# State sums by accumulating DMAs, a third of the C products off VectorE, and a new order of pieces in a tuned scan-and-attention kernel

## The chip, the cores and the metric

The kernel runs on one core of a Trainium2 chip. The metric is the device time of one execution in microseconds (us). A kernel's time is the median of its runs, with the lowest and highest beside it. Engines are named as in the profile: PE is TensorE, PEld its weight loads, DVE is VectorE, ACT is ScalarE, POOL is GpSimd, and SP is SyncE, which here only issues transfers.

## The reference, cut to what matters

The input is 4 images of 4096 positions with 96 channels. One block follows another:

```python
# layer 0: a selective scan with 16 states per channel
x = x + conv(GroupNorm(x))
#   xf = LayerNorm(...) * gamma + beta
#   value, gate, delta, A, B, C = split(xf @ W_in + b_in)   # A, B, C: 96 x 16 columns each
#   h = d * A * h + d * B * u          (d = delta, u = value, along the 4096 positions)
#   y = sigmoid(gate) * sum over 16 states (C * h);   y @ W_out + b_out
# layer 1: linear attention and a feed-forward net, rounded to 8 and 16 bit floats
t = t + attention(LayerNorm(t));  t = t + ffn(LayerNorm(t))
```

The kernel cuts an image into 8 chunks of 512 positions, and a chunk into 12 tiles of 128 (channel, state) pairs: 4 sets of states by 3 groups of 32 channels. One tile is one step, so there are 32 chunks and 384 steps.

## The kernel before

Each step has a fixed core, and the other work ("pieces") is dealt out to the 12 positions of a chunk.

```python
# one step s (cut): A, B, C projections on PE; B's copy on ACT and product on POOL;
# A's product, the scan and C's product on DVE
tiles[s + 1].a_proj();  tiles[s].c_proj();  last.keep()
tiles[s + 1].b_mul()                       # POOL
last = tiles[s];  last.scan()              # DVE
tiles[s + 1].a_mul()                       # DVE
last.c_mul()                               # DVE
call(s)                                    # the pieces dealt to this step
tiles[s + 2].b_proj();  tiles[s + 2].b_copy()
...
# state_sum (cut): 4 sets x 3 groups x 2 passes of a matmul with a folding matrix, one set every 3 steps
# LayerNorm (cut): a product of 128 x 4 elements on DVE, both inputs in SBUF
nc.vector.scalar_tensor_tensor(nmr, self.mv[:, :, 0], -1.0, self.r, ALU.mult, ALU.mult)
...
# front (cut): x is split into a high part xs and a rest lo; lo reads PSUM and one SBUF input
nc.scalar.activation(v["xs"][0:C, :], v["ps"], AF.Copy, scale=gam)
nc.vector.scalar_tensor_tensor(lo, v["ps"], gam, v["xs"][0:C, :].bitcast(F32), ALU.mult, ALU.subtract)
...
# tail (cut): the transposed chunk, 97 rows of 512, stays in SBUF until attention a whole image later
xat[b, i] = big.tile([CA, J, P], F32, tag="xat", name=f"xat_{nm}", bufs=NCH + 2)
nc.scalar.copy(xat[b, i], v["ps"])
```

An image's x is loaded once and kept, also for the GroupNorm of the image that comes next.

Of the kernel before, what the change touches and what calls it, by code (L numbers as in the profile page):

```python
# [38 lines left out]
GN0, GN_EVERY = 22, 6  # L39
FFN0 = 15  # L40
XBUFS = 2 * NCH + 5
# [4 lines left out]
def conv_attn_hybrid_kernel(  # L46
# [27 lines left out]
    psum = ctx.enter_context(tc.tile_pool(name="psum", bufs=1, space=PSUM))  # L74

    BANKS = {"A": 2, "B": 1, "C": 1, "Y": 1, "M": 2, "G": 1}

    def bank(tag, shape, name):
        return psum.tile(shape, F32, tag=tag, name=name, bufs=BANKS[tag])

# [8 lines left out]
    xt = {}  # L89

    def load_x(b, i):
        t = big.tile([P, J, C], F32, tag="x", name=f"x_{b}_{i}", bufs=XBUFS)
        nc.sync.dma_start(t, x_v[b, i])
        xt[b, i] = t
# [3 lines left out]


# [4 lines left out]
    raw0 = big.tile([C, A0], F32, tag="x", name="raw0", bufs=XBUFS)  # L104
    nc.scalar.dma_start(raw0, w_in[:, 0:A0])
    raws, brows = {}, {}
    for k, c0 in enumerate((B0, A0, C0)):
        for cg in range(NCG):
            t = big.tile([C, 32 * S], F32, tag="xat", name=f"raw{k}{cg}", bufs=NCH + 2)
            n0 = c0 + cg * 32 * S  # L110
            nc.scalar.dma_start(t, w_in[:, n0 : n0 + 32 * S])
            raws[k, cg] = t
        brows[k] = work.tile([NCG, 32 * S], F32, tag="ch", name=f"brow{k}", bufs=6)
        nc.scalar.dma_start(
            brows[k], b_in[c0 : c0 + C * S].rearrange("(g n) -> g n", g=NCG)
        )
    b_dug = const.tile([C, 3], F32, name="b_dug")
    for k in range(3):
        nc.scalar.dma_start(b_dug[:, k : k + 1], b_in[k * C : (k + 1) * C].unsqueeze(1))

# [24 lines left out]






    def split_high(dst, src):

        nc.scalar.copy(dst[0:C, 0], src)

    def split_low(dst, src, engine):
        engine.tensor_tensor(dst[0:C, 1], src, dst[0:C, 0].bitcast(F32), ALU.subtract)

    def split_copies(dst):
        v = dst.bitcast(F32)
        nc.sync.dma_start(v[C:P, 0], v[64:C, 0])  # L160
        nc.sync.dma_start(v[C:P, 1], v[64:C, 1])
        nc.sync.dma_start(v[0:64, 2], v[0:64, 0])
        nc.sync.dma_start(v[64:P, 2], v[0:64, 1])

    def split_rows(xs, xl, lo):

        nc.sync.dma_start(xl[0:64, :].bitcast(F32), lo[0:64, :].bitcast(F32))
        nc.sync.dma_start(xl[64:P, :].bitcast(F32), lo[0:64, :].bitcast(F32))
        nc.sync.dma_start(xs[C:P, :].bitcast(F32), lo[64:C, :].bitcast(F32))

    def project(ps, wt, split):

        xs, xl = split
        for n, mv in enumerate((xs, xs, xl)):
            nc.tensor.matmul(ps, lhsT=wt[:, n], rhs=mv, start=(n == 0), stop=(n == 2))  # L175


    bets = const.tile([P, 2], F32R, name="bets")
    betl = const.tile([P, 2], F32R, name="betl")
    betlo = const.tile([C, 2], F32R, name="betlo")  # L180
    nc.scalar.copy(bets[0:C, :], bet.to_broadcast([C, 2]))
    nc.gpsimd.tensor_tensor(
        betlo, bet.to_broadcast([C, 2]), bets[0:C, :].bitcast(F32), ALU.subtract
    )
    split_rows(bets, betl, betlo)

    w_dug = const.tile([P, 3, 3 * C], F32R, name="w_dug")
    split_high(w_dug, raw0)
    split_low(w_dug, raw0, nc.gpsimd)
    split_copies(w_dug)  # L190
    w_bac = [const.tile([P, 3, NCG, NSH * P], F32R, name=f"w_{k}") for k in range(3)]
    b_bac = const.tile([P, 3, NCG, NSH], F32, name="b_bac")

    def cols(k, cg):

        return (
            w_bac[k][:, :, cg].rearrange("k n (s c) -> k n s c", s=S),
            raws[k, cg].rearrange("k (c s) -> k s c", s=S),
        )

    def high(k):
        for cg in range(NCG):
            split_high(*cols(k, cg))

    def low(k, engine):
        for cg in range(NCG):
            split_low(*cols(k, cg), engine)
        split_copies(w_bac[k].rearrange("k n g c -> k n (g c)"))

    def bias_dug():  # L210
        ps = bank("Y", [C, 3, 2], "dug_ps")
        for k in range(3):
            project(ps[:, k], w_dug[:, :, k * C : (k + 1) * C], (bets, betl))
        nc.vector.tensor_tensor(b_dug, b_dug, ps[:, :, 0], ALU.add)


    betd = []
    for nm, t in (("s", bets), ("l", betl)):
        m = const.tile([P, NCG, 4], F32R, name=f"betd_{nm}")
        nc.gpsimd.memset(m.bitcast(F32), 0.0)  # L220
        for cg in range(NCG):
            nc.gpsimd.tensor_copy(m[:, cg, cg : cg + 1], t[:, 0:1].bitcast(F32))
        betd.append(m)

    def bias(k):
        ps = bank("Y", [4, NSH * P], f"bias_ps{k}")
        for cg in range(NCG):
            for n, t in enumerate((betd[0], betd[0], betd[1])):
                nc.tensor.matmul(
                    ps, lhsT=t[:, cg, :], rhs=w_bac[k][:, n, cg],  # L230
                    start=(cg == 0 and n == 0), stop=(cg == NCG - 1 and n == 2),
                )
        row = work.tile([NCG, NSH * P], F32, tag="ch", name=f"bias{k}", bufs=6)
        nc.vector.tensor_tensor(
            row.rearrange("g (s c) -> g s c", s=S),
            ps[0:NCG].rearrange("g (s c) -> g s c", s=S),
            brows[k].rearrange("g (c s) -> g s c", s=S), ALU.add,
        )
        t_ps = bank("C", [P, NSH, NCG], f"biast_ps{k}")
        for sh in range(NSH):  # L240
            nc.tensor.transpose(
                t_ps[:, sh, :], row[:, sh * P : (sh + 1) * P], ident[:NCG, :NCG]
            )
        nc.vector.tensor_copy(b_bac[:, k], t_ps.rearrange("p h g -> p g h"))


    w_o = const.tile([CA, C], F32, name="w_o")
    nc.scalar.dma_start(w_o[0:C, :], w_out)
    nc.scalar.dma_start(w_o[C:CA, :], b_out.unsqueeze(0))
    w_qkv = const.tile([CA, 3 * C], F32, name="w_qkv")  # L250
    nc.scalar.dma_start(w_qkv[0:C, :], wqkv)
    nc.scalar.dma_start(w_qkv[C:CA, :], bqkv.unsqueeze(0))
    w_ff = const.tile([C, C], F32, name="w_ff")
    nc.scalar.dma_start(w_ff, wff)

    w_qt = const.tile([CA, CA], F32, name="w_qt")
    kvff = const.tile([CA, C], F32, name="kvff")
    nc.scalar.dma_start(kvff[C:CA, :], bff.unsqueeze(0))
    w1_q = const.tile([C, HID], F8, name="w1_q")
    w2_q = const.tile([P, NK, C], F8, name="w2_q")  # L260
    b1_q = const.tile([P, NK], F32, name="b1_q")
    b2_q = const.tile([P, C], F32, name="b2_q")
    w1_sb = big.tile([P, NK, C], F32, tag="x", name="w1_sb", bufs=XBUFS)
    nc.scalar.dma_start(w1_sb, w1.rearrange("(m p) k -> p m k", p=P))
    w2_sb = big.tile([C, HID], F32, tag="x", name="w2_sb", bufs=XBUFS)
    nc.scalar.dma_start(w2_sb, w2)
    b1_sb = big.tile([NK, P], F32, tag="x", name="b1_sb", bufs=XBUFS)
    nc.scalar.dma_start(b1_sb, b1.rearrange("(m p) -> m p", p=P))
    b2_sb = big.tile([P, C], F32, tag="x", name="b2_sb", bufs=XBUFS)
    nc.scalar.dma_start(b2_sb, b2.partition_broadcast(P))  # L270

    def weights_attention():
        nc.gpsimd.memset(w_qt[C:CA, :], 0.0)
        nc.gpsimd.memset(w_qt[C:CA, C:CA], 1.0)
        ps = bank("Y", [C, CA], "wq_ps")
        nc.tensor.transpose(ps, w_qkv[:, 0:C], ident[:CA, :CA])
        nc.vector.tensor_copy(w_qt[0:C, :], ps)

    def weights_ffn1():
        ps = bank("Y", [C, HID], "w1_ps")  # L280
        for m in range(NK):
            nc.tensor.transpose(ps[:, m * P : (m + 1) * P], w1_sb[:, m, :], ident)
        nc.vector.tensor_copy(w1_q, ps, saturate=False)

    def weights_ffn2():
        ps = bank("Y", [P, NK, C], "w2_ps")
        for m in range(NK):
            nc.tensor.transpose(ps[:, m, :], w2_sb[:, m * P : (m + 1) * P], ident[:C, :C])
        nc.vector.tensor_copy(w2_q, ps, saturate=False)

    def weights_bias():
        ps = bank("Y", [P, NK], "b1_ps")
        nc.tensor.transpose(ps, b1_sb, ident[:NK, :NK])
        b1_8 = small.tile([P, NK], F8, tag="b1_8", name="b1_8", bufs=1)
# [10 lines left out]
    for r in range(2):  # L305
        t = const.tile([P, J, CA], F32, tag=f"xa{r}", name=f"xa{r}")
        nc.gpsimd.memset(t[:, :, C:CA], 1.0)
        xa_t.append(t)


    fold = const.tile([P, 32], F32, name="fold")

    hmask = []

# [611 lines left out]
```

## Time and profile before

| | before |
|---|---|
| median of 3 runs | 1439.53 us (1438.23 to 1440.04) |
| span of the profiled run, granted TensorE clock | 1435.1 us, 0.951 |
| first scan starts | 71.1 us |
| last scan starts, time from there to the end | 1347.5 us, 88 us |
| transfers that PE waits for inside the loop | none |

A group line reads: line, engine, operation, output<-inputs, shapes, count, then busy us in all and mean ns of one, then the idle time of the engine just before these instructions and who ended it. The prediction below shows the main groups. Two groups of DVE instructions that it doesn't show matter later:

```profile
L521 DVE SCALAR_TENSOR_TENSOR lo<-xnt_ps,gam,xs 96x512 fp32r<-96x512 f32 x32 | 23.6, 738 | 1.6 <-ACT xs L516 1.6
L350 DVE SCALAR_TENSOR_TENSOR nmr_c<-mv_c,rstd_c 128x4 f32<-128x4 f32 x32 | 5.4, 169 | 1.0 <-POOL rstd_c L328 1.0
```

The first takes 738 ns for 512 columns and has one of its two large inputs in PSUM (xnt_ps). The second takes 169 ns for 4 columns, with both inputs in SBUF.

### The profile page before, as it was taken

To read this page: it belongs to the slowest core of one execution; us is meant where nothing else is said; L and a number is where in the kernel's file an instruction comes from. 1 tells how busy PE (TensorE), PEld (TensorE's weight loads), DVE (VectorE), ACT (ScalarE), POOL (GpSimd) and SP (SyncE) were. 2 spreads that over 40 slices of the span, in tenths; PEclk is the share of its full clock that TensorE was granted. 3 is DMA by queue.
4 is the path that set the end of the run, shared out by engine and by line. 5 is a ranking of instruction groups with operands and counts; after the bars stand their busy time and mean duration, and the time that the engine had idled before them with its cause. 6 is when DMAs were issued, how large, how long until landed. Compare 5 with 4: busy or idle time off the path is not lost. (4 is left out here: it accounts for less than half of the span.)

```text
span 1435.1 us, 20740 instructions
## 1 busy us (share of the span) xinstructions
PE 1300.3 (91%) x6396; PEld 891.0 (62%) x6396; DVE 1212.5 (84%) x2309; ACT 723.1 (50%) x1658; POOL 747.2 (52%) x743
## 2 busy tenths in 40 slices
PE   2699988899999899899999998989999999999885
PEld 2356665666666666666666666666666666666562
DVE  2398988899998898899998888889999999999742
ACT  3234343433336555555555455665554555655555
POOL 3254544455554555555555555555556566545424
PEclk6699999999999999999999999999999999999955
DMA  6422222222222222222222122222222222222001
GB/s 156 107 61 56 49 55 61 48 54 54 54 59 51 69 51 56 57 47 60 60 50 70 45 62 57 58 52 58 59 49 49 51 60 59 50 49 51 12 6 44
DMA packets 81357, 80.98 MB, mean 56 GB/s; under 512 B 49617, under 2 KB 50101, under 8 KB 81246
## 3 DMA queue, kind: packets, MB, share of 16 engines
q1 hardware_dynamic: 78544, 77.22, 22.6%
q10 hardware_dynamic: 2702, 2.43, 0.7%
q8 instruction: 51, 0.84, 0.3%
q14 instruction: 60, 0.49, 0.1%
HBM read 8.72 MB, written 6.29 MB: 10 GB/s over the span
## 5 line engine op out<-in xcount | busy, mean ns | idle before, releaser
L598 POOL TENSOR_TENSOR bu<-bu,du 128x512 f32<-128x512 f32 x384 | 493.9, 1286 | 575.2 <-ACT bu L595 351.2
L614 DVE TENSOR_TENSOR_SCAN h<-Aps,state,bu 128x512 f32<-128x512 f32 x336 | 428.1, 1274 | 46.6 <-POOL bu L598 45.4
L595 ACT ACTIVATE bu<-Bps,b_bac 128x512 f32<-128x512 f32 x384 | 261.8, 682 | 398.2 <-PE Bps L175 386.2
L607 DVE SCALAR_TENSOR_TENSOR Aps<-Aps,b_bac,d 128x512 f32<-128x512 f32 x384 | 284.3, 740 | 64.5 <-PE Aps L175 63.8
L175 PE MATMUL Bps<-xs,w 128*128 128x512 f32 x768 | 271.0, 434 | 52.7 <-ACT gx_ps L412 37.6
L632 DVE SCALAR_TENSOR_TENSOR ch<-Cps,b_bac,h 128x512 f32<-128x512 f32 x384 | 285.5, 744 | 1.5 <-PE Cps L175 1.3
L175 PE MATMUL Cps<-xs,w 128*128 128x512 f32 x768 | 245.0, 401 | 3.0 <-DVE ch L632 2.9
L175 PE MATMUL Aps<-xs,w 128*128 128x512 f32 x768 | 241.7, 396 | 2.4 <-DVE h L614 2.1
L175 PEld LDWEIGHTS Bps<-xs,w 128*128 128x128 f32 x768 | 127.4, 191 | 102.1 <-ACT gx_ps L412 44.8
L175 PEld LDWEIGHTS Cps<-xs,w 128*128 128x128 f32 x768 | 142.1, 190 | 46.4 <-DVE ch L632 17.9
L175 PEld LDWEIGHTS Aps<-xs,w 128*128 128x128 f32 x768 | 145.4, 190 | 38.0 <-DVE h L614 4.1
L175 PE MATMUL Bps<-xl,w 128*128 128x512 f32 x384 | 152.6, 397 | 0.0
L175 PE MATMUL Aps<-xl,w 128*128 128x512 f32 x384 | 151.9, 395 | 0.0
L175 PE MATMUL Cps<-xl,w 128*128 128x512 f32 x384 | 151.6, 395 | 0.0
L645 PE MATMUL y_ps<-ch,fold 128*32 128x512 f32 x768 | 136.5, 605 | 0.0
L354 ACT ACTIVATE xa<-x,nmr_a,rstd_a 128x96 f32<-128x96 f32 x128 | 49.4, 457 | 105.0 <-DVE nmr_a L350 105.0
L354 ACT ACTIVATE z<-z,nmr_c,rstd_c 128x96 f32<-128x96 f32 x128 | 49.4, 457 | 78.1 <-DVE nmr_c L350 78.1
L175 PEld LDWEIGHTS Aps<-xl,w 128*128 128x128 f32 x384 | 72.8, 190 | 16.9
L175 PEld LDWEIGHTS Bps<-xl,w 128*128 128x128 f32 x384 | 72.6, 189 | 16.9
L175 PEld LDWEIGHTS Cps<-xl,w 128*128 128x128 f32 x384 | 72.8, 189 | 16.5
L787 ACT ACTIVATE hq<-hr 128x512 fp8e5<-128x512 f16 x96 | 60.6, 631 | 17.9 <-PE y_ps L793 8.2
L614 DVE TENSOR_TENSOR_SCAN h<-Aps,bu 128x512 f32<-128x512 f32 x48 | 58.1, 1211 | 11.0 <-POOL bu L598 10.9
(163 smaller groups left out, 1594.3 us busy)
## 6 DMA issues: line engine op xcount, KB each, us to landing
d<-d SPq DMA_DIRECT2D x384, 64.0 KB, 2.0
du<-du SPq DMA_DIRECT2D x384, 64.0 KB, 2.0
xl<-lo SPq DMA_DIRECT2D x64, 128.0 KB, 2.3
x<-in_x_dram SPq DMA_DIRECT2D x32, 192.0 KB, 2.8
out_dram<-o SPq DMA_DIRECT2D x32, 192.0 KB, 2.2
w<-w SPq DMA_DIRECT2D x6, 384.0 KB
xs<-lo SPq DMA_DIRECT2D x32, 64.0 KB, 2.0
raw<-in_L_conv_W_in_dram ACTq DMA_DIRECT2D x9, 192.0 KB, 4.5
```

The source lines that it names most:

```text
L175: nc.tensor.matmul(ps, lhsT=wt[:, n], rhs=mv, start=(n == 0), stop=(n == 2))
L354: nc.scalar.activation(dst[:, j, 0:C], src[:, j, :], AF.Identity, bias=nmr[:, j : j + 1], scale=self.r[:, j : j + 1],)
L595: nc.scalar.activation(self.bu, self.b_ps, AF.Identity, bias=self.bias(0))
L598: nc.gpsimd.tensor_tensor(self.bu, self.bu, rep["du4", self.b, self.i, self.cg], ALU.mult)
L607: nc.vector.scalar_tensor_tensor(self.a_ps, self.a_ps, self.bias(1), rep["d4", self.b, self.i, self.cg], ALU.add, ALU.mult,)
L614: nc.vector.tensor_tensor_scan(self.h, self.a_ps, self.bu, 0.0 if self.i == 0 else state[self.sh, self.cg], ALU.mult, ALU.add,)
L632: nc.vector.scalar_tensor_tensor(self.ch, self.c_ps, self.bias(2), self.h, ALU.add, ALU.mult)
L645: nc.tensor.matmul(y_ps[g][cg * 32 : (cg + 1) * 32, :], lhsT=fold, rhs=tiles.pop(g * NT + NCG * sh + cg).ch, start=(sh == 0), stop=(sh == ...
L787: nc.scalar.activation(v["hq"][:, m, :], v["hr", m], AF.Copy, saturate=False)
```

## The change

The intent is to take work off the two engines that are nearly full. State sets are added by DMA instead of by PE, four of twelve C products move from DVE to ACT and POOL, and the pieces are dealt anew. To make room in SBUF for the larger C tiles, two things that had stayed in SBUF now travel: x is loaded twice (once for GroupNorm as `gx`, once for the rest), and the transposed chunk `xat` is written to memory and read back. The diff, cut to its core:

```diff
+ON_POOL = (1, 3, 6, 10)
-XBUFS = 2 * NCH + 5
+XBUFS = 14
 ...  # state sums: three of four sets by DMA
+    def gather(g, sh):
+        nc.gpsimd.dma_start(chs[g, 0], chs.pop((g, sh)), accum_op=ALU.add)
+            for n, sh in ((6, 1), (10, 2), (13, 3)):
+                    at(s0 + n, gather, g, sh)
+        at(s0 + 4, state_sum, g)          # now one set, in the next chunk
 ...  # C product of positions 1, 3, 6, 10
+        def c_copy(self):   nc.scalar.activation(self.ch, self.c_ps, AF.Identity, bias=self.bias(2))
+        def c_mul_pool(self):   nc.gpsimd.tensor_tensor(self.ch, self.ch, self.h, ALU.mult)
 ...  # the transposed chunk leaves SBUF and comes back
-            xat[b, i] = big.tile([CA, J, P], F32, tag="xat", ...)
-            nc.scalar.copy(xat[b, i], v["ps"])
+        def spill():
+            d = xat[b, i] = dram.tile([CA, J, P], F32, tag="xat", ...)
+            nc.sync.dma_start(d, v["xat"])
+        at(s0 + 16, spill)
+        def fetch():
+            v["xa"] = sb("xal", [CA, J, P], F32, f"xal_{nm}")
+            nc.sync.dma_start(v["xa"], xat.pop((b, i)))
 ...  # x loaded twice: for GroupNorm (gx), and again for the front
+        at(when[0] - 5, load_x, b, 0, gxt, "gx")
+                at(max(when[n] - 4, when[n - 1]), load_x, b, n, gxt, "gx")
+        at(s - 3, load_x, b, i)
 ...  # front: one more ACT copy; the subtraction now reads two SBUF tiles
+            nc.scalar.activation(self.xf, self.ps, AF.Identity, scale=gam, bias=bet)
+            nc.scalar.copy(self.xs[0:C, :], self.xf)
+            nc.vector.tensor_tensor(lo, self.xf, xs[0:C, :].bitcast(F32), ALU.subtract)
 ...  # B leads by one step more
-        if 0 <= s + 1 < K:
-            tiles[s + 1].b_mul()
+        if 0 <= s + 2 < K:
+            tiles[s + 2].b_mul()
+        if 0 <= s + 3 < K:  tiles[s + 3].b_proj();  tiles[s + 3].b_copy()
```

Not shown are the new prologue (GroupNorm of the first image ahead of the weight splits), GroupNorm's sums moved to the shared PSUM banks, and the last image's feed-forward net with one quantisation instead of three.

## The prediction

> **What bounds the kernel now.** The work is 32 chunks (four images of eight), each of 12 scan steps; a step projects A, B and C of one tile, multiplies, scans, and the other pieces (front, tail, FFN, GroupNorm of the next image) are dealt out among the steps. I read the busy line first, then the groups.
>
> ```profile
> PE 1300.3 (91%) x6396; PEld 891.0 (62%) x6396; DVE 1212.5 (84%) x2309; ACT 723.1 (50%) x1658; POOL 747.2 (52%) x743
> ...
> L598 POOL TENSOR_TENSOR bu<-bu,du 128x512 f32<-128x512 f32 x384 | 493.9, 1286 | 575.2 <-ACT bu L595 351.2
> L614 DVE TENSOR_TENSOR_SCAN h<-Aps,state,bu 128x512 f32<-128x512 f32 x336 | 428.1, 1274 | 46.6 <-POOL bu L598 45.4
> L595 ACT ACTIVATE bu<-Bps,b_bac 128x512 f32<-128x512 f32 x384 | 261.8, 682 | 398.2 <-PE Bps L175 386.2
> L607 DVE SCALAR_TENSOR_TENSOR Aps<-Aps,b_bac,d 128x512 f32<-128x512 f32 x384 | 284.3, 740 | 64.5 <-PE Aps L175 63.8
> ...
> L632 DVE SCALAR_TENSOR_TENSOR ch<-Cps,b_bac,h 128x512 f32<-128x512 f32 x384 | 285.5, 744 | 1.5 <-PE Cps L175 1.3
> ...
> L645 PE MATMUL y_ps<-ch,fold 128*32 128x512 f32 x768 | 136.5, 605 | 0.0
> ```
>
> DVE is idle little, and waits in two places only: 64 us for A from PE, 57 us for B's product from POOL. PE and DVE both look nearly full, but these durations overlap their neighbours, so I took what each instruction really holds its engine, from start to next start in the timeline:
>
> ```profile
> 707.81 1.21 DVE L614 TENSOR_TENSOR_SCAN h<-Aps,bu 128x512 f32<-128x512 f32 x1
> ...
> 708.84 1.06 PE L645 MATMUL y_ps<-ch,fold 128*32 128x512 f32 x6
> ...
> 710.24 1.21 DVE L614 TENSOR_TENSOR_SCAN h<-Aps,bu 128x512 f32<-128x512 f32 x1
> ...
> 722.87 0.62 PE L175 MATMUL Bps<-xs,w 128*128 128x512 f32 x2
> ...
> 723.56 0.62 PE L175 MATMUL Aps<-xs,w 128*128 128x512 f32 x2
> ```
>
> A projection of three matmuls holds PE 0.69 us (722.87 to 723.56), so A, B, C are 2.07 a step; a state sum holds it 1.0. Scan, A product and C product hold DVE 2.43 together, as 1.13 to 1.20, 0.64, 0.66. The first scan starts at 71.1, the last ends at 1348.8: prologue 71, loop 1278, drain 86. By the starts of each chunk's first scan a chunk takes 36.1 us without FFN and GroupNorm, 39.1 with FFN, 41 to 42.5 with both.
>
> I then summed by step, from the code, what is dealt to each of the 12 positions, and took the larger of PE and DVE at each. The pieces' holds, again by starts: on PE a group of four transposes 0.44, an output or attention product 0.9, a d/u/gate projection 0.69, a hidden layer 0.23, the FFN's output 0.52, the Gram product 0.5; on DVE the statistics of a LayerNorm 0.9, lo and du 0.66 each, the gating 0.6, a residual 0.46. Position 3, for example, has on PE 2.07 + 1.0 + 0.9 = 4.0 (state sum, attention), on DVE 2.5 + 0.46 = 3.0, so it counts 4.0. PE and DVE march step by step, because C has one PSUM bank and A two. An FFN chunk gives PE 36.0 and DVE 36.0 in all, but the sum of the step maxima is 39.4 (measured 39.1); without FFN 37.4 (measured 36.1). So the bound is neither engine alone: it is the heavier of the two in each step, with at most a step of slack. GroupNorm adds some 3 us, as its transposes share B's only bank.
>
> The ends of the run:
>
> ```profile
> 28.10 0.57 POOL L443 TENSOR_TENSOR gm<-gv,mhalf 96x1 f32<-96x1 f32 x1
> ...
> 69.76 1.28 POOL L598 TENSOR_TENSOR bu<-bu,du 128x512 f32<-128x512 f32 x1 [6.29 <-DMA du<-du]
> ...
> 1401.77 0.63 ACT L787 ACTIVATE hq<-hr 128x512 fp8e5<-128x512 f16 x1 [2.44 <-PE y_ps L793]
> 1407.39 0.63 ACT L787 ACTIVATE hq<-hr 128x512 fp8e5<-128x512 f16 x1 [1.12 <-PE y_ps L793]
> ...
> du<-du SPq DMA_DIRECT2D x384, 64.0 KB, 2.0
> ```
>
> GroupNorm's last value was ready to compute at 15.4, but POOL took it at 28.1, after weight splits; du's copies end the prologue. In the drain a chunk repeats every 5.6 to 6.9 us, in waits to and fro between PE, ACT and DVE.
>
> **What the Trainium skill says.** "Trainium Kernel Development and Optimization", Performance Expectations, calls matmul busy time a bad metric since matmuls are pipelined; the trace agrees: 0.39 us matmuls start 0.23 apart. "DMA: Bandwidth & Descriptors", SWDGE vs HWDGE vs iDMA, has accumulating DMAs only from GpSimd, with descriptors made in software there; no run yet shows what that costs POOL. The same page, Anatomy of one DMA, fits a transfer as about 2.0 us plus bytes over 436 GB/s; the 64 KB copies' 2.0 us agrees with the fixed part. "SBUF — State Buffer", Who interferes with whom, has a DVE instruction with two SBUF inputs contend with POOL's reads; the scan and both products have one input in PSUM, so the added POOL work should not slow them.
>
> **The change part by part.** (1) State sums: four sets a chunk become one, three 768 KB accumulating DMAs taking their place. PE loses 3 x 1.0 = 3.0 us a chunk, about 100 us in all. The DMA is an estimate from the fit: 2.0 + 1.8, and as it reads two operands say 5.5 to 6. They are issued at positions 6, 10 and 13, each must wait for the one before, and the sum stands at 16: three or four steps of about 3 us between them, so they should land in time. Traffic rises by 95 x 0.79 = 75 MB, about doubling 81 MB, at 24% use of the DMA engines now.
>
> (2) Four C products leave DVE: 4 x 0.66 = 2.6 us a chunk, 85 us in all. ACT gains 4 x 0.58 = 2.3, POOL 4 x 1.24 = 5.0 plus three DMA issues of perhaps 1. An FFN chunk's POOL total becomes 27.6 + 3 = 31, ACT's about 25.
>
> (3) B is projected three steps ahead instead of two, and its product leads by two instead of one: the 57 us that scans wait for POOL, and the head-of-line waits for bu, should nearly go. GroupNorm moves to the three shared M banks, one sum a chunk, so its 3 us should fall to about 1. One more ACT copy (xf) is 32 x 0.58, hidden.
>
> (4) New order. By the same unit costs, at positions 0 to 11 of an FFN chunk (base 2.07 on PE; 2.5 on DVE, 1.84 at positions 1, 3, 6, 10 whose C product leaves), DVE gets 2.5, 1.8, 2.5, 1.8, 4.1, 3.1, 2.5, 3.9, 3.4, 2.7, 1.8, 3.2 (33.3) and PE 2.5, 2.3, 3.2, 3.0, 3.1, 3.2, 3.0, 2.6, 2.6, 2.5, 3.2, 2.1 (33.3). The maxima sum to 37.5, without FFN to 35.9. But heavy PE steps (3, 10) now stand beside heavy DVE ones (4, 11), so a step of slack evens out 1.5 to 2.5: I take 35.5 and 34.3. FFN starts 29 steps after its image, so some 10.4 chunks lack it: 10.4 x 34.3 + 21.6 x 35.5 = 1124. For waits I cannot see (GroupNorm's M banks, POOL late) I add 0.8 a chunk: 1150, against 1278.
>
> (5) Prologue. Without the bias matmuls, and with GroupNorm's root ahead of the splits, I follow: statistics done about 11, spread 16.5, first chunk normalised on DVE 21, transposed and split 24, copies landed 28.5, du 31.5, its first copies 38.5, first scan about 40. But the third weight's copies stand behind 24 of d and du on the SP queue (0.62 us each), landing near 50, and the first C projection waits for them: worth a first scan at 47. So 47 instead of 71.
>
> (6) Drain. ACT per chunk falls: three quantisations of 0.54 become one (about 1.5), y16 goes to DVE: about 3.8 us; DVE gets about 4.1. The period should be near 5, which saves some 10 us; but image 2's last FFN now begins 14 steps later and falls into the drain, which gives a few back: 80 instead of 86.
>
> Sum: 47 + 1150 + 80 = 1277; with 2 us between profile and clock, 1278.
>
> **Rivals.** First, the accumulating DMA is slow: if it takes over 9 us, PE stands at every state sum. For it: two reads for one write, and nothing measured here. Against it: DMA engines are 24% busy, and the spacing of 4, 3, 3 steps looks chosen. Three us late each chunk makes 32 x 3 = 96 us: 1375. Second, POOL becomes the bound: at 3 us an issue its chunk is 27.6 + 9 = 36.6, and since it works in order, a wait for an earlier DMA blocks B's product: about 1320. Third, PE and DVE even out fully: 33.3 and 31 a chunk make the loop about 1050, total 1177; the present loop never did (36 of work, 39.1 measured). Fourth, the ACT copy of C at its step's end holds the only C bank: 128 x 0.5 us would make 1340.
>
> **Range and chances.** The two ends are worth -30, give or take 12; the loop -128, give or take 40, where the spread is mostly the evening-out and the DMA. Hence 1230 to 1330. Over 2% faster (below 1411) fails only if two rivals join: 0.94; within 2% 0.04; slower 0.02.
>
> **What would show it.** Chunks of 34 to 36.5 us by their scans; y_ps down to about 200 matmuls; DVE's C products x256; DVE's wait for POOL's bu below 25 us; each accumulating DMA landing under 9 us and PE not waiting for one ahead of y_ps; POOL's issue about 1 us; first scan near 40 with a stall of some us after it; last scan to end about 80. Wrong if POOL is over 90% busy in the loop, or y_ps waits on a DMA in every chunk.

## The result, and the profile after

The changed kernel took 1798.55 us (1793.64 to 1799.86, 4 runs) against 1438.88 us (1438.02 to 1440.04) for the kernel before on the same chip. The ratio is 1.249, with a 95% interval of 1.247 to 1.252. A ratio here is the mean time of one kernel's fast runs over that of the other's fast runs of the same rounds, so it is not quite the ratio of the medians. The prediction was 1278 us: wrong in direction, and by 520 us in size.

Busy times and groups of the kernel after, with the same columns as before:

```profile
PE 1268.4 (71%) x5782; PEld 926.5 (52%) x5782; DVE 1205.0 (67%) x2189; ACT 819.6 (46%) x1789; POOL 983.2 (55%) x955
...
L573 POOL TENSOR_TENSOR bu<-bu,du 128x512 f32<-128x512 f32 x384 | 510.8, 1331 | 414.0 <-ACT state L599 207.7
L582 DVE SCALAR_TENSOR_TENSOR Aps<-Aps,b_bac,d 128x512 f32<-128x512 f32 x384 | 284.8, 742 | 430.8 <-PE Aps L224 430.6
...
L589 DVE TENSOR_TENSOR_SCAN h<-Aps,state,bu 128x512 f32<-128x512 f32 x336 | 426.2, 1268 | 9.8
...
L353 PE MATMUL gx_ps<-ident,gx 128*96 128x128 f32 x96 | 23.3, 391 | 273.2 <-DMA gx<-in_x_dram 273.2
...
L613 DVE SCALAR_TENSOR_TENSOR ch<-Cps,b_bac,h 128x512 f32<-128x512 f32 x256 | 190.1, 743 | 2.5 <-PE Cps L224 2.4
...
L628 POOL DMA_DIRECT2D ch<-ch x95 | 85.3, 898 | 31.3 <-DVE ch L613 15.6
```

What the change set out to do, it did. DVE has 256 C products instead of 384. The scans wait 9.8 us instead of 46.6, so B's longer lead works. The matmuls of the state sums fell from 768 to 198. But no engine is near full any more: DVE fell from 84% to 67% of a longer span, and it waits 430 us for A from PE. PE in turn stands 273 us before a group of 96 small transposes, of `gx`, and what ends that is a transfer. The view of waits, of PE and of POOL, says it in one line each (us in all, times, longest):

```profile
PE gx_ps L353 <- DMA gx<-in_x_dram: 273.2, 20, 16.8
PE a_ps L753 <- DMA xal<-xatd: 66.2, 27, 8.0
...
POOL z L465 <- DMA x<-in_x_dram: 84.5, 24, 30.6
```

All three are transfers that the kernel before did not have or did not wait for. A load of x took 2.8 us there from issue to landing. What makes one last 14 us is seen in the timeline of one such wait (start, duration, engine):

```profile
884.39 2.49 SPq L513 DMA_DIRECT2D du<-du  x4
...
886.98 0.38 SPq L676 DMA_DIRECT2D xatd<-xat  x1
...
887.41 0.83 SPq L105 DMA_DIRECT2D gx<-in_x_dram  x1
...
901.91 1.06 PE L353 MATMUL gx_ps<-ident,gx 128*96 128x128 f32 x4 [16.84 <-DMA gx<-in_x_dram]
```

The load of gx is issued 0.4 us after the spill of xat and is usable 14.5 us later. The view of windows of the same stretch shows what the machine does meanwhile. Its columns are the busy us of PE, PEld, DVE, ACT and POOL with their counts, then the granted clock, the share of the 16 DMA engines that is busy, and GB/s:

```profile
890.00:896.00 6.00, 0.00 (x0) 0.00 (x0) 0.00 (x0) 0.00 (x0) 0.00 (x0) 0.50 0.71 143
896.00:900.00 4.00, 0.00 (x0) 0.00 (x0) 0.00 (x0) 0.00 (x0) 0.00 (x0) 0.50 0.06 20
```

Every compute engine is idle for 10 us. In the first 6 us the accumulating DMA is running. In the last 4 us the DMA share is 0.06, which is one engine of sixteen. The trace's packet records say which packets these are:

```text
packets on the SP queue, kernel after, number started in each us and mean duration
889: 453 of 384 B (gx), 25 ns      7 of 2048 B
891:                              12 of 2048 B, 84 ns   (beside 31 accumulating packets of 6144 B)
894 to 897:                        1 to 4 of 2048 B a us, 91 to 98 ns
898:                              13 of 2048 B, 84 ns
899:                              12 of 2048 B, 84 ns
900 to 901: 32 of 384 B (gx), 22 ns   10 of 2048 B, 84 ns, then no more
```

A 2048-byte packet is one row of the spilled tile: 4 x 128 x 4 bytes. (The table is cut: 890, 892 and 893 are left out.) Twelve a us at 84 ns each is one after another, as on a single engine, and all 97 rows are 97 x 84 ns = 8.1 us. Nearly all of gx had moved by 890; its last 32 packets, which are 512 / 16 or one engine's share, came when the rows were through. The Trainium skill has the rule, in "DMA: Bandwidth & Descriptors", section "Why a DMA increments its semaphore by 16 and not by 1": the number of engines used is the largest up to 16 that divides the slowest dimension on both sides, so that 127 partitions or a single scalar get 1, and 96 or 128 get 16. The tile has 97 partitions, and 97 is prime. The 0.06 and the 84 ns agree.

The chain that ended last, as shares of the span, shows the same on the way back, in the drain: the fetch of 97 partitions stands ahead of attention in every chunk.

```profile
DMA xal<-xatd 4%; PE a_ps L753 1%; POOL yb L817 0%; POOL o L823 0%; PE y_ps L638 0%; POOL rstd_f L313 0%; ACT xn L323 0%; DVE h L788 0%; DVE st_f L305 0%; DVE nmr_f L317 0%; PE Cps L224 0%; ACT xa L323 0%; PE h_ps L775 0%; DVE ch L613 0%; DVE h L589 0%
```

By the starts of the scans, most chunks that carry the next image's GroupNorm take 53 to 57 us, those of the last image, which carry none, 38 to 42. The first scan starts at 71.9 us, and from the start of the last one to the end are 139 us (before: 71.1 and 88). The granted TensorE clock was 0.840, against 0.951 before; it rose again in the runs below as the waits went (0.922 in e1, 0.945 in g2). Just after the wait above, two matmuls of a projection take 1.20 us, and 5 us later 0.71. So part of what a wait costs may be slower PE work after it. No run separates this part.

One small group had grown as well, from 169 to 1433 ns for its 4 columns:

```profile
L317 DVE SCALAR_TENSOR_TENSOR nmr_c<-mv_c,rstd_c 128x4 f32<-128x4 f32 x31 | 44.4, 1433 | 1.5 <-POOL rstd_c L313 1.5
```

### The profile page after: what moved, and what is told of

The parts are those of the page before. It is cut to its first block, busy times and chain, and to the rows that moved or that the text cites. A ratio compares the mean times of both kernels' runs of the same rounds, so it can differ in the third digit from the quotient of the medians.

```text
span 1797.3 us, 19737 instructions
## 1 busy us (share of the span) xinstructions
PE 1268.4 (71%) x5782; PEld 926.5 (52%) x5782; DVE 1205.0 (67%) x2189; ACT 819.6 (46%) x1789; POOL 983.2 (55%) x955
## 5 line engine op out<-in xcount | busy, mean ns | idle before, releaser
L573 POOL TENSOR_TENSOR bu<-bu,du 128x512 f32<-128x512 f32 x384 | 510.8, 1331 | 414.0 <-ACT state L599 207.7
L589 DVE TENSOR_TENSOR_SCAN h<-Aps,state,bu 128x512 f32<-128x512 f32 x336 | 426.2, 1268 | 9.8
L224 PE MATMUL Bps<-xs,w 128*128 128x512 f32 x768 | 290.4, 461 | 26.8 <-ACT bu L570 26.7
L224 PE MATMUL Aps<-xs,w 128*128 128x512 f32 x768 | 262.8, 425 | 44.4 <-DVE h L589 43.6
L224 PE MATMUL Cps<-xs,w 128*128 128x512 f32 x768 | 264.6, 427 | 20.4 <-DVE ch L613 17.0
L353 PE MATMUL gx_ps<-ident,gx 128*96 128x128 f32 x96 | 23.3, 391 | 273.2 <-DMA gx<-in_x_dram 273.2
L622 POOL TENSOR_TENSOR ch<-ch,h 128x512 f32<-128x512 f32 x128 | 173.8, 1358 | 63.3 <-ACT ch L619 61.3
L613 DVE SCALAR_TENSOR_TENSOR ch<-Cps,b_bac,h 128x512 f32<-128x512 f32 x256 | 190.1, 743 | 2.5 <-PE Cps L224 2.4
L353 PEld LDWEIGHTS gx_ps<-ident,gx 128*96 128x96 f32 x96 | 14.5, 176 | 282.4 <-issue 215.8
L619 ACT ACTIVATE ch<-Cps,b_bac 128x512 f32<-128x512 f32 x128 | 87.6, 684 | 52.2 <-PE Cps L224 52.1
L628 POOL DMA_DIRECT2D ch<-ch x95 | 85.3, 898 | 31.3 <-DVE ch L613 15.6
L753 PE MATMUL a_ps<-rmat,xal 97*128 97x96 f32 x256 | 44.6, 330 | 68.9 <-DMA xal<-xatd 66.2
```

The costliest lines, as they stand in the source:

```text
L224: nc.tensor.matmul(ps, lhsT=wt[:, n], rhs=mv, start=(n == 0), stop=(n == 2))
L353: nc.tensor.transpose(self.ps[:, j * P : (j + 1) * P], self.src[self.b, n][:, j, :], ident)
L573: nc.gpsimd.tensor_tensor(self.bu, self.bu, rep["du4", self.b, self.i, self.cg], ALU.mult)
L589: nc.vector.tensor_tensor_scan(self.h, self.a_ps, self.bu, 0.0 if self.i == 0 else state[self.sh, self.cg], ALU.mult, ALU.add,)
L613: nc.vector.scalar_tensor_tensor(self.slot(), self.c_ps, self.bias(2), self.h, ALU.add, ALU.mult)
L619: nc.scalar.activation(self.ch, self.c_ps, AF.Identity, bias=self.bias(2))
```

## The experiments

The main theory was that the 97-partition transfers, each on one DMA engine, stop the SP queue. The rivals were that the accumulating DMAs fill the DMA engines, or that the order of the SP queue is at fault and the size of the spill is not. Twelve runs were made, all with correct results. The kernel before ran beside each batch, at medians of 1440.14, 1440.16, 1439.05 and 1440.17 us.

| run | us (lowest to highest) | ratio to before, 95% interval |
|---|---|---|
| after | 1798.55 (1793.64 to 1799.86) | 1.249 (1.247 to 1.252) |
| e1_spread | 1490.48 (1487.17 to 1495.59) | 1.036 (1.032 to 1.039) |
| e2_order | 1562.96 (1560.49 to 1563.13) | 1.085 (1.083 to 1.087) |
| e3_nogather | 1724.1 (1722.06 to 1725.01) | 1.197 (1.195 to 1.200) |
| e4_spread_nogather | 1549.71 (1543.48 to 1550.96) | 1.075 (1.072 to 1.078) |
| f2_gxearly | 1413.44 (1412.36 to 1414.13) | 0.982 (0.980 to 0.983) |
| f3_all | 1375.02 (1371.96 to 1378.08) | 0.955 (0.953 to 0.957) |
| f4_all_nopool | 1348.32 (1344.47 to 1349.83) | 0.936 (0.934 to 0.938) |
| f6_shift_pool | 1394.39 (1387.09 to 1398.27) | 0.968 (0.965 to 0.970) |
| g1_nopool_nogather | 1430.81 (1430.65 to 1431.19) | 0.995 (0.993 to 0.996) |
| g2_shift_pool_lo_ps | 1316.81 (1310.6 to 1318.82) | 0.915 (0.912 to 0.917) |
| g4_two_pool | 1349.38 (1348.55 to 1353.47) | 0.939 (0.936 to 0.941) |
| h1_shift_lo_ps_nopool | 1336.23 (1334.57 to 1336.5) | 0.928 (0.926 to 0.929) |

**e1_spread.** The spill and the fetch, each cut into 96 partitions and 1:

```diff
-            nc.sync.dma_start(d, v["xat"])
+            nc.sync.dma_start(d[0:C], v["xat"][0:C])
+            nc.sync.dma_start(d[C:CA], v["xat"][C:CA])
-            nc.sync.dma_start(v["xa"], xat.pop((b, i)))
+            d = xat.pop((b, i))
+            nc.sync.dma_start(v["xa"][0:C], d[0:C])
+            nc.sync.dma_start(v["xa"][C:CA], d[C:CA])
```

> The changed kernel with one edit: the spill and the fetch of the 97-partition tile are each cut into 96 partitions and one. Theory (a DMA over 97 partitions runs on a single DMA engine, 97 packets of 2 KB at 84 ns = 8.1 us, and all later transfers of the SP queue stand behind it on that engine): the wait of PE for the GroupNorm load (273 us now) falls below 40 us, the wait for the fetched tile (66 us) below 15, the fetch lands in under 4 us, drain from the last scan falls from 139 to 80-95 us; time 1300 to 1390 us. Rival (the accumulating DMAs crowd out the other transfers): the load still lands late and the time stays above 1600 us.

Splitting two transfers took 308 us away (1798.55 to 1490.48). The direction was right; the size that I expected was too large. PE's waits for the fetch are gone, the drain fell from 139 to 96 us, and the wait for gx fell from 273 us, though not to zero:

```profile
PE gx_ps L353 <- DMA gx<-in_x_dram: 72.2, 20, 11.7
```

So the 97 partitions are the main cause, but a second one stands behind them.

**e2_order.** The kernel after with its spill whole, but two steps later, so that gx is issued ahead of it:

```diff
-        at(s0 + 16, spill)
+        at(s0 + 18, spill)
```

> The changed kernel, only the spill issued two steps later, so that the GroupNorm load stands before it in the SP queue and not behind it; the spill still runs on one engine. Theory of the queue behind the spill: PE's wait for the GroupNorm load falls from 273 to below 100 us, the drain stays near 139 us, time 1450 to 1580 us. Rival (accumulating DMAs crowd it out): no change, above 1700 us.

1562.96 us: PE's wait for gx fell to 63.4 us with the slow spill still there, while the wait for the fetch (68.5 us) and the drain (139 us) stayed. So the spill costs what it costs because a load that PE needs stands behind it in the same queue. In e2 the spill is as slow as before, but gx stands ahead of it, and PE waits no longer for gx than in e1 (72.2 us). The savings of e1 and e2 (308 and 236 us) overlap and must not be added.

**e3_nogather and e4_spread_nogather.** The kernel after, and e1, without accumulating DMAs. All four sets are summed on PE in one step:

```diff
-                if g < N - 1 or sh < NSH - 1:
-                    at(s0 + n, gather, g, sh)
+                pass
-        at(s0 + 4, state_sum, g)
-        at(s0 + 5, gated)
+        at(s0 + 1, state_sum, g)
+        at(s0 + 2, gated)
```

> The changed kernel without the 95 accumulating DMAs; the four state sets of a chunk are summed on PE again, in one go at position 13. Spill and fetch unchanged. Theory of the single engine: the spill still takes 97 x 84 ns = 8 us with nothing beside it, so PE still waits some 8 to 10 us a GroupNorm chunk for the load; time 1600 to 1740 us, drain still over 125 us. Rival (accumulating DMAs are the cause): below 1480 us.

> Both edits: spill and fetch spread over the engines, and no accumulating DMAs. If the sums on PE cost what the step count says (3 x 1.0 us a chunk, and in one burst of 4 us), it is 60 to 110 us slower than e1_spread, about 1380 to 1480 us. If the accumulating DMAs cost more than they save, it is as fast as e1_spread or faster.

e3 gave 1724.1 us: without any accumulating DMA, PE still waits 218 us for gx. That rival falls as the main cause. But 74 us go with the accumulating DMAs. One likely reason is in the packet records above: the rows' rate falls from 12 to between 1 and 4 a us while accumulating packets, by these rates, share their engine. Another was not separated from it: in e3 the small product nmr_c takes 150 ns instead of 1433 (see f4). In the spread version the sign turns round: e4 is 59 us slower than e1, at the lower edge of the 60 to 110 that I had expected. So there the accumulating DMAs are a gain over four sums in one step; the kernel before had the sums spread (see g1).

**f2_gxearly.** e1, with the loads of gx two steps earlier. In e1's timeline the 24 small copies of d and du, with the spill after them, take 21 us to issue on the SP queue (724 to 745 us in one chunk), and gx stood behind them:

```diff
-        at(when[0] - 5, load_x, b, 0, gxt, "gx")
+        at(when[0] - 7, load_x, b, 0, gxt, "gx")
-                at(max(when[n] - 4, when[n - 1]), load_x, b, n, gxt, "gx")
+                at(max(when[n] - 6, when[n - 1]), load_x, b, n, gxt, "gx")
```

> e1_spread with the GroupNorm load issued two steps earlier, ahead of the 24 copies of d and du in the SP queue. Theory (in e1_spread the load is late only because it stands behind those copies, which take 21 us to issue): PE's wait for it falls from 72 to under 15 us, GroupNorm chunks from about 42.5 to 39.5 us, time 1395 to 1445 us. Rival (the chunks with GroupNorm are slow from its work on ACT and in the M banks): chunks stay above 41.5 us, time above 1470 us.

1413.44 us, 77 less, and now 1.8% below the kernel before. PE's wait for gx fell from 72.2 to 11.9 us, all of it one wait in the first chunk. What is left of the queue besides that is mostly POOL's wait for the second load of x, 98.3 us against 97.8 in e1:

```profile
POOL z L465 <- DMA x<-in_x_dram: 98.3, 27, 30.9
```

**f3_all.** f2, with the front's x loaded eight steps earlier, and the first image's x not loaded a second time, since the prologue already holds it:

```diff
-XBUFS = 14
+XBUFS = 15
-        "x": XBUFS, "gx": 2, ...
+        "x": XBUFS, "gx": 1, ...
-        at(s - 3, load_x, b, i)
+        if b:
+            at(s - 11, load_x, b, i)
```

> f2_gxearly, and the loads of x: image 0's are not loaded a second time, the others' are issued eight steps earlier, ahead of the copies (one more x buffer, one less for GroupNorm's). Theory: POOL's wait for x (98 us in e1_spread, 31 of it before the first scan) falls below 15 us, the first scan starts at 52 to 60 instead of 72 us, time 30 to 60 us below f2_gxearly, 1350 to 1410. Rival (those waits of POOL were hidden): within 10 us of f2_gxearly.

1375.02 us, another 38 less. The first scan starts at 53.1 us instead of 72.8. The 30.9 us above were in the prologue: chunk 1's x, loaded a second time, stood behind the 24 copies of the first chunk and the third weight's copies, and POOL did B's first products only after it (x was there at 59.1, the first product began at 66.1 us).

**f4_all_nopool.** f3 with all twelve C products on DVE:

```diff
-ON_POOL = (1, 3, 6, 10)
+ON_POOL = ()
```

> f3_all with all twelve C products on DVE again. By the list of steps, the four steps without one take 2.05 us each and would take about 2.5, so it is 1.6 us a chunk, 50 us in all, slower than f3_all. Rival (POOL, with 5 us a chunk more work, holds up DVE instructions that read two SBUF operands, the 4-element products of the LayerNorms at 0.4 to 1.7 us against 0.15 to 0.25 before, so the four products gain nothing): within 15 us of f3_all or faster, with those instructions back below 0.5 us.

1348.32 us: putting 128 products of 741 ns back on DVE makes the kernel 27 us faster. My first theory, that the move saves DVE time and so kernel time, falls for this version. In f3 the small LayerNorm product behaves as in this line, and in f4 as in the next (mean ns is the second number after the first bar):

```profile
L317 DVE SCALAR_TENSOR_TENSOR nmr_c<-mv_c,rstd_c 128x4 f32<-128x4 f32 x31 | 34.9, 1125 | 1.5 <-POOL rstd_c L313 1.5
```

```profile
L317 DVE SCALAR_TENSOR_TENSOR nmr_c<-mv_c,rstd_c 128x4 f32<-128x4 f32 x31 | 6.2, 201 | 1.5 <-POOL rstd_c L313 1.5
```

With POOL's added products it takes 1125 ns, without them 201, for the same four columns. A mean hides the spread: in f3 the shortest takes 165 ns, the median 231 and the longest 3504. The products alone are not enough, though. In e3, with all four of them on POOL but no accumulating DMAs, the same group reads:

```profile
L317 DVE SCALAR_TENSOR_TENSOR nmr_c<-mv_c,rstd_c 128x4 f32<-128x4 f32 x31 | 4.6, 150 | 1.5 <-POOL rstd_c L313 1.5
```

In e3's timeline the product stands in a gap of POOL, between a product of B and one of C. In the 11 cases of f3 that take over 1 us, two or three POOL products run back to back over it, and it ends within some 40 ns of the last of them.

**f6_shift_pool.** f3, with that product, in all three LayerNorms, moved to POOL itself, which has just computed its input:

```diff
-            nc.vector.scalar_tensor_tensor(self.nmr, self.mv[:, :, 0], -1.0, self.r, ALU.mult, ALU.mult)
+            nc.gpsimd.tensor_scalar(self.nmr, self.mv[:, :, 0], -1.0, None, ALU.mult)
+            nc.gpsimd.tensor_tensor(self.nmr, self.nmr, self.r, ALU.mult)
# and ln.shift one or two steps earlier, beside rstd
```

> f3_all with the LayerNorms' 4-element product (mean times 1/std) computed on POOL, right after 1/std, and not on DVE. Theory (DVE stands still[...]: 65 us more than before in these 87 instructions): DVE loses these waits and the time falls by 40 to 65 us against f3_all. Rival (the waits fall where DVE would wait for PE anyway): within 15 us of f3_all.

A miss: 1394.39 us, 19 slower than f3 where I had expected a gain. The profile shows why. In the timeline of one chunk, DVE and POOL:

```profile
697.39 5.62 DVE L489 TENSOR_TENSOR lo<-xf,xs 96x512 fp32r<-96x512 f32 x1 [0.55 <-ACT xs L484]
```

```profile
697.56 2.75 POOL L573 TENSOR_TENSOR bu<-bu,du 128x512 f32<-128x512 f32 x2
700.03 1.13 POOL L628 DMA_DIRECT2D ch<-ch  x1
700.65 1.81 POOL L573 TENSOR_TENSOR bu<-bu,du 128x512 f32<-128x512 f32 x1
```

The subtraction lo, 0.69 us elsewhere, is held for 5.62 us while POOL runs one instruction after another, and ends soon after the last of them (703.0 against 702.5); DVE's next scan starts at 702.9. This is the longest case. Of the 32, 15 took their 0.69 us, and the other 16 took 3.15 to 3.50. Over the whole run lo's mean rose from 764 (f3) to 2174 ns:

```profile
L489 DVE TENSOR_TENSOR lo<-xf,xs 96x512 fp32r<-96x512 f32 x32 | 69.6, 2174 | 15.0 <-ACT xs L484 15.0
```

The hold-up had not gone; it had passed to the next DVE instruction that reads two SBUF tiles. The Trainium skill says in "SBUF — State Buffer", section "Who interferes with whom", that such an instruction contends with a POOL instruction that reads SBUF. These runs agree, and the change itself made lo one of that kind: before, lo read PSUM.

**g2_shift_pool_lo_ps.** f6, with lo reading PSUM again. ACT writes its result back to the bank:

```diff
-            self.xf = sb("xf", [C, TC], F32, f"xf_{self.nm}")
-            nc.scalar.activation(self.xf, self.ps, AF.Identity, scale=gam, bias=bet)
+            nc.scalar.activation(self.ps, self.ps, AF.Identity, scale=gam, bias=bet)
+            self.xf = self.ps
```

> The run with LayerNorm's 4-element product on POOL (1394 us), in which the subtraction lo, with both inputs in SBUF, took 2.17 us; here lo reads one input from PSUM (ScalarE writes xf back to the bank instead of to SBUF). If an instruction of VectorE with two SBUF inputs is what POOL's work holds up, lo comes back to 0.65 to 0.9 us and the time falls by 15 to 45 us (1350 to 1380 us). If lo was slow for another reason (it waits for ScalarE's copy, or for the PSUM bank now held longer), lo stays over 1.5 us and the time stays above 1385 us.

1316.81 us, 78 less than f6, more than I had expected, and the fastest of all: 8.5% below the kernel before. lo is back:

```profile
L489 DVE TENSOR_TENSOR lo<-xnt_ps,xs 96x512 fp32r<-96x512 f32 x32 | 21.9, 685 | 13.5 <-ACT xs L484 13.1 <-DMA du<-du 0.5
```

The instruction's work is the same; only where one input lies, and so where ACT writes it, has changed.

**h1_shift_lo_ps_nopool.** g2 with all C products on DVE, which completes a square:

```diff
-ON_POOL = (1, 3, 6, 10)
+ON_POOL = ()
```

> The fourth corner: as the run of 1317 us (LayerNorm's small product on POOL, lo reading PSUM) but with all twelve C products on VectorE. In the versions whose small instructions read two SBUF inputs, moving four products to ScalarE and POOL cost 27 us (1375 against 1348 us). If those small instructions were what took the gain away, the same move is now a gain, so this run is slower than 1317 us by 15 to 50 us (1332 to 1367 us). If the gain of the 1317 us run came only from the small product's place and not from the products, this run is 1290 to 1315 us.

| | four C products on ACT and POOL | all on DVE |
|---|---|---|
| nmr and lo on DVE with two SBUF inputs | 1375.02 (f3) | 1348.32 (f4) |
| nmr on POOL, lo reads PSUM | 1316.81 (g2) | 1336.23 (h1) |

The same move of products costs 27 us in the upper row and gains 19 in the lower. The theory held, for the two instructions together; no run moves lo alone.

The gain is still far below the 85 us that DVE was relieved of. The means of the 12 positions, from scan to scan over chunks 4 to 30 (counted from 0), show why. From h1 to g2, positions 1, 3, 6 and 10 get shorter by 0.46, 0.30, 0.61 and 0.21 us, but positions 4 and 11 get longer, from 4.51 to 5.01 and from 3.65 to 4.02. In the timeline of g2, the scan that opens position 4 and DVE's next instruction:

```profile
650.93 1.22 DVE L589 TENSOR_TENSOR_SCAN h<-Aps,bu 128x512 f32<-128x512 f32 x1
...
653.08 0.76 DVE L582 SCALAR_TENSOR_TENSOR Aps<-Aps,b_bac,d 128x512 f32<-128x512 f32 x1 [0.92 <-PE Aps L224]
```

DVE gets to this scan sooner because position 3's product has left it. Then it waits 0.92 us for A, because PE is still working through what was dealt to position 3 (the value projection and a hidden layer), and then B's projection. Shortening one engine's step moves the wait to the other engine.

**g4_two_pool.** f3 with two products moved instead of four:

```diff
-ON_POOL = (1, 3, 6, 10)
+ON_POOL = (1, 6)
```

> As the run with spread spills and early loads, but only two of twelve C products (positions 1 and 6) on ScalarE and POOL instead of four (1375 us) or none (1348 us). If POOL's work costs in proportion, 1355 to 1368 us. If there is an optimum between (VectorE 91% busy without any, POOL's collisions with four), it is faster than 1348 us, 1325 to 1345 us. The product of four elements (nmr, first LayerNorm) should lie between 0.2 and 1.1 us.

1349.38 us, the same as f4 with none (1348.32), and 26 below f3. nmr_c still takes 1112 ns, but the second LayerNorm's product is back at 267. Neither of my two ranges was met: the cost is not in proportion to the number of products, and there is no optimum between. With e3 this suggests that it depends on which of POOL's instructions lies beside which small DVE instruction. No run moves one POOL instruction alone to show it.

**g1_nopool_nogather.** f4 without the accumulating DMAs, by the same edit as e3:

> The run with spread spills, early loads and all C products on VectorE (1348 us), with the accumulating DMAs taken out: the four sets of C products are summed on TensorE again. If the accumulating DMAs are a real gain also once the queue is in order, this is 35 to 75 us slower (1383 to 1423 us; the same removal cost 59 us in the spread version). If the gain was only that TensorE had no slack while it waited for late loads, it stays within 15 us of 1348.

1430.81 us, 82 slower than f4, just over what I had expected. The 82 us probably overstate what the accumulating DMAs are worth, as in this version all four sums stand in one step, and position 2 takes 6.05 us instead of 2.64, while the kernel before spread them over the chunk.

## Why the prediction was wrong, point by point

**The step that failed first is one that is not there.** The sum "47 + 1150 + 80" has no term for the new transfers on the SP queue. Part (1) counted the bytes of the accumulating DMAs and set them against "24% use of the DMA engines now". The 32 spills and 32 fetches of 97 partitions were not costed at all. They occupy one engine for 8.1 us each, and what is issued behind them lands behind them. Spreading them was worth 308 us (e1). An average of 24% over sixteen engines told nothing about one engine.

**"GroupNorm moves to the three shared M banks ... so its 3 us should fall to about 1"** (part 3). The PSUM bank was indeed no longer the limit (before, PE waited 37.6 us for ACT to free it; after, this wait is not in the list), but gx is a transfer that had not existed before, issued 4 steps ahead into a queue that was busy for some seven steps. Chunks with GroupNorm became 12 to 15 us longer than the last image's, instead of 1. After the spreading, its early issue was worth another 77 us (f2).

**"First scan about 40"** with a stall "worth a first scan at 47" (part 5). Measured: 71.9. I followed the weights and the normalisation, and overlooked that the first image's x is loaded again and that POOL waits 30.6 us for it. With that mended (f3) the first scan is at 53.1, and its chunk takes 53.5 us, some 17 more than the next ones. Of these, two waits of PE in f3 make up 17.0:

```profile
PE gx_ps L353 <- DMA gx<-in_x_dram: 11.7, 1, 11.7
PE Cps L224 <- DMA w<-w: 5.3, 1, 5.3
```

The stall that I had named, the third weight's copies, is the smaller one, under the 7 us that I gave it. The larger is the missing term again: in the first chunk gx is issued at 88.7 us, behind 24 copies of d and du, and f2's earlier place did not remove that wait.

**"The scan and both products have one input in PSUM, so the added POOL work should not slow them"** (the paragraph on the skill). True as it stands: scan, A product and C product took 1268, 742 and 743 ns after, against 1274, 740 and 744 before. But I asked the question only of the large instructions. The products of four elements and the new lo are of the kind that is blocked, and DVE's next instruction had to wait for them. f3 to g2 gives their worth, 58 us.

**"A step of slack evens out 1.5 to 2.5: I take 35.5 and 34.3"** (part 4). In e1 the last image's chunks took 37.5, the sum of the maxima that I had worked out (the rounded list as printed adds up to 37.7), so no net evening-out was left. Heavy PE positions 2, 3, 6 and 10 did come out shorter than their maxima, but positions 4 and 11 came out at 5.1 and 5.2 instead of 4.1 and 3.2. Once nmr and lo were no longer held up, position 11 fell to 4.0, and in g2 most of the last image's chunks took 35.7 to 36.3, most of the early ones without the feed-forward net 34.0 to 34.9. So the size of this term was about right, for a kernel in which these small instructions are not blocked. Its place was not, so the size is in part luck. In g2's last image (chunks 24 to 30) the pairs that were to even out took 7.3 us (positions 3 and 4) and 6.0 (10 and 11), where their maxima add up to 7.1 and 6.4; most of the gain came at positions 1, 2 and 6.

**"80 instead of 86"** for the drain (part 6). That counts from the end of the last scan. Measured from its start, which adds 1.2, it was 139 after, as each fetch takes 8 us there, and 96 once they were spread (97 in g2). What makes the remaining 15 or so was not isolated by a run. In f4's timeline the last image's first attention starts 35 us after the start of the last scan, where the kernel before needed 21, so the image 2 work that "falls into the drain" is the likely cause.

**What held.** The accumulating DMA lands after 7.2 us (the profile's list of transfers), under the 9 us of the first rival though over my estimate of 5.5 to 6. Its issue holds POOL 0.9 us, as guessed, and PE waited 4.9 us in all for one. B's longer lead did what part (3) said. POOL stayed below its bound, at 55% after and 78% in g2.

**What the difference adds up to.** From 1798.6 to 1278 are 520.6 us. In the order tried: spreading the spill and fetch 308, gx ahead of the copies 77, x ahead and not reloaded 38, nmr and lo 58. In another order the shares would differ, as e2 shows. What is left is g2's span of 1317.1 against the 1277 of the sum, and it lies at the ends. In g2 the first scan starts at 53.0, the first chunk takes 52.6, the other 31 take 1115.5 up to the end of the last scan (36.0 each), and the drain from there 96.0. The prediction had 47, then 32 chunks of 1150 / 32 = 35.9, then 80. So prologue and first chunk are 105.6 instead of 82.9 (23 more, of which PE waits 11.7 for gx and 5.7 for the third weight), the drain is 16 more, and the 31 chunks are within 2 us. That last agreement leans on the 0.8 us a chunk added for waits not seen: most of g2's chunks take 33.9 to 36.3, but five near the ends of images take 37.7 to 41.0.

## What to carry to other kernels

When a change moves a tile out of SBUF, cost that transfer as carefully as the compute that it makes room for. Look first at whether its partition count has a large divisor up to 16, and then at what is issued behind it on the same queue. When work is given to POOL, look through DVE's list for every instruction that reads two SBUF tiles, the tiny ones too, before counting the gain. A change that loses can hold a real gain: here the same idea, with its transfers spread and ordered and two small inputs moved, went from 25% slower to 8.5% faster.

## What the Trainium skill lacked or had wrong

- "DMA: Bandwidth & Descriptors", section "Why a DMA increments its semaphore by 16 and not by 1", has the rule by which 97 partitions get one engine, and the runs agree (0.06 of 16 engines busy, 84 ns per 2048-byte row, 308 us by splitting 96 + 1). Its section "Queues, rings and completion order" has that each engine takes its descriptors in ring order. What neither spells out is what follows for a queue: a later load that uses all engines is not usable until the one engine is through (gx issued at 887.4, used at 901.9, against 2.8 us for such a load before).
- The page's fit in section "Anatomy of one DMA" gave my 3.8 us for 768 KB. The accumulating DMA from SBUF to SBUF measured 7.2 us after and 6.7 us in e1, with 6144-byte packets of about 490 ns. I found no figure for the time of an accumulating DMA on the page. That another queue's rows slow down meanwhile (from 12 to between 1 and 4 a us) is no gap: the page says that an engine takes turns between its queues packet by packet, but not that such a packet takes about 490 ns. The fit is given for transfers that POOL issues; the prediction set the 64 KB copies, which SP issues, beside it.
- "SBUF — State Buffer", section "Summary: rules for kernel authors", says that the second to issue is blocked until the first finishes, which reads as a wait for one instruction of the other. These runs show a longer hold: lo lasted 5.62 us in f6 across four POOL instructions back to back (two products of B, a DMA issue, another product), 3.15 to 3.50 in 16 other cases, and a product of four columns up to 3.5 us in f3, where 0.69 and 0.15 us are its undisturbed times.
